# Weaving counted in TensorE's work, with a lag for each piece, and the scan's pair sum behind the second scan

## The chip, the cores and the metric

The kernel runs on one core of a Trainium2 chip. The metric is the time of one execution in microseconds on the device. The names in this text are those of the profile: PE is TensorE (matmuls, with PEld its weight loads), DVE is VectorE, ACT is ScalarE, POOL is GpSimd, and SP is SyncE, which here only issues DMAs. A line such as L539 is a line of the kernel before the change.

## The reference, cut to what matters

Eight samples of 512 tokens with 128 channels go through two layers, both with adaptive layer normalisation.

```python
# layer 0, for each of 8 samples x (512 x 128)
h  = LN(x) * (1 + ca) + sa
xn = LN(h) * ln1_w + ln1_b
#   causal attention, 16 heads of 8 channels
s  = mask(q @ k.T * 8 ** -0.5);  attn = softmax(s) @ v @ o_w + o_b
#   state space branch: 256 channels, 16 states
x_ssm, z = split(xn @ in_proj_w)
x_c = silu(causal_conv4(x_ssm));  dt = softplus(...);  Bm, Cm = ...
for t: state = exp(dt[t] * A) * state + (x_c[t] * dt[t]) * Bm[t]
       y[t] = sum over the 16 states of Cm[t] * state
ssm = ((y + x_c * D) * silu(z)) @ ssm_out_w
h  = h + alpha * attn + (1 - alpha) * ssm
h  = h + gelu(LN(h) @ ffn_w1) @ ffn_w2          # biases left out
x  = x + ga * h
hm = LN(x) * (1 + cb) + sb
#   mixture of experts: a shared one, and the 2 best of 8 by a router
logits = relu(hm @ Wr1) @ Wr2
x  = x + gb * (expert_shared(hm) + sum over e of weight[e] * expert_e(hm))
# layer 1: at each token, attention over the 8 samples (8 heads),
# then a channel mix: sigmoid(xr @ W_r) * (relu(xk @ W_k)**2 @ W_v)
```

An expert is `silu(hm @ W1 + b1) @ W2 + b2` with a hidden width of 512. All eight experts are computed for all tokens, and weighted with zeros where they were not chosen.

## The kernel before

All activations lie with the 128 channels on the partitions and the 512 tokens of one sample along the free axis. A loop over the samples b runs layer 0 as a software pipeline. Each stage is a Python generator which emits some instructions (a piece) and then yields a cost, a number that stands for the time of the piece. The function `weave` (L201) takes several such generators, each with a total cost and a stretch of the turn, for example 0 to 0.83, and always advances the one that is least far along its stretch. So the order of all instructions on PE, ACT and DVE is written out by hand, since the loop stands in a manual schedule for these three engines. POOL and SP are left to the framework's scheduler. Each engine executes its instructions in the order written and waits at an instruction until its operands are there.

In turn b these generators are woven:

- `attention(b)`: for each of four groups g of four heads, `projections` (queries and keys, L465 to L476), `maxima` (raw scores, L488 and L496, and their maximum on DVE, L520, into `mpad`), `shifts` (the negated maxima are transposed by TensorE as `mT`, L534, and added to the queries on DVE, L539), `exponentials` (scores again, now shifted, as `e` at L488, the mask added at L496, and the exponential on ACT, L558), `values` (L572), and `projected` (denominators L591, their reciprocal `rd` on DVE L599, broadcast by TensorE at L604, output projection L619 and L628).
- `ssm_scan(b)`, within 0 to 0.83 of the turn. It has 16 units, each of two states for half of the 256 channels. A unit has a product on DVE (`hs`, L783), two scans on DVE (L788), and a product with Cm on POOL (L792). The two states of the unit before are added by a pair sum on DVE (L764), and then to the running sum on POOL (L765). ACT computes the decays (L750). The tile `hs` has three buffers, the decays four, and the broadcast Bm and Cm rows, which SP loads by DMA, two each. `paced` ties each piece of the scan behind the DVE instruction of the attention that was marked last.
- `head(b+1)`: load, the first normalisation `lna`, and a second one, `ln1`.
- `attention2(b-2)`: layer 1's attention for one sample: a normalisation `lnc`, keys and values (L313, L320), queries (L329), and products and sums on POOL and DVE (L348 to L393).
- `ssm_inputs(b+1)` and the first seven pieces of `attention(b+1)`, at the turn's end.
- `finish(b-1)`: `tail`, which is the normalisation `ln2`, the feed-forward part (L834, L838), the normalisation `lnb` which gives `hm` (L283), and `routing` (first matmul L864); then `experts`, with nine experts of four matmuls L945, silu L949, four matmuls L960, and the weighted sum on DVE (`wb`, L968) and POOL (L971). The weights `wb` come by DMA (L957). L975 closes the sample.

A normalisation (`normalised`, L242 to L276) is a chain that leaves TensorE and returns three times: centring matmul L242, square and copy on ACT (L245, L247), variance matmul L254, addition of epsilon on DVE (L263), power -1/2 on POOL (L264), broadcast matmul L269, product on DVE (L276).

In PSUM there are three one-bank buffers for most matmuls, two for scores, and one accumulator.

Of the kernel before, what the change touches and what calls it, by code (L numbers as in the profile page):

```python
# [17 lines left out]
P = 128  # L18
# [5 lines left out]
NG = NH // 4  # L24
# [43 lines left out]
CST, NCST = _cols(_CONST)  # L68
MSK, NMSK = _cols(_MASK)


@with_exitstack
def kernel(
# [126 lines left out]
    def weave(*parts):  # L200

        live = []
        for k, (pieces, whole, begin, end) in enumerate(parts):
            live.append([begin, k, iter(pieces), (end - begin) / whole])
        while live:
            part = min(live)
            cost = next(part[2], None)
            if cost is None:  # L210
                live.remove(part)
            else:
                part[0] += cost * part[3]

# [22 lines left out]
    def normalised(src, name, lane, cost=0.9, n=T, ring=mm_tile, wait=0.0):  # L237


        mps = ring(f"{name}_m")[:, :n]  # L240
        to = mps if len(src.shape) == 2 else mps.rearrange("p (a b) -> p a b", a=src.shape[1])
        nc.tensor.matmul(to, lhsT=centre, rhs=src, start=True, stop=True)  # L242
        yield 0.2
        sq = lnp.tile([P, T], F32, tag=f"ln_s{lane}", name=f"{name}_s")
        nc.scalar.activation(sq[:, :n], mps, AF.Square)  # L245
        d = lnp.tile([P, T], F32, tag=f"ln_d{lane}", name=f"{name}_d")[:, :n]
        nc.scalar.copy(d, mps)  # L247
        yield 2 * cost - 0.2


        vps = ring(f"{name}_v")
        blocks = [(k, min(k, n - P)) for k in range(0, n, P)]
        for j, (_, lo) in enumerate(blocks):
            nc.tensor.matmul(  # L254
                vps[:, j : j + 1],
                lhsT=sq[:, lo : lo + P],
                rhs=mean_w,
                start=True,
                stop=True,
            )  # L260
        sd = lnp.tile([P, NTT], F32, tag=f"ln_r{lane}", name=f"{name}_r")
        nj = len(blocks)
        nc.vector.tensor_scalar(sd[:, :nj], vps[:, :nj], EPS, None, ALU.add)  # L263
        nc.gpsimd.tensor_tensor(sd[:, :nj], sd[:, :nj], mhalf[:, :nj], ALU.pow)  # L264
        yield cost + wait

        rps = ring(f"{name}_rb")
        for j, (k, lo) in enumerate(blocks):
            nc.tensor.matmul(  # L269
                rps[:, k : lo + P],  # L270
                lhsT=sd[:, j : j + 1].to_broadcast([P, P]),
                rhs=ident[:, k - lo :],
                start=True,
                stop=True,
            )
        nc.vector.tensor_mul(d, d, rps[:, :n])  # L276
        yield cost
        return d

    def layernorm(dst, src, scale, bias, name, lane, cost=0.9, n=T, ring=mm_tile, wait=0.0):  # L280

        d = yield from normalised(src, name, lane, cost, n, ring, wait)
        nc.scalar.activation(dst, d, AF.Identity, bias=bias, scale=scale)  # L283
        yield cost

# [16 lines left out]
    def attention2(s, at):  # L302
# [6 lines left out]
        for i0 in range(0, NB, 2):  # L309
# [14 lines left out]
            )  # L324
            yield 0.9
        ps = mm_tile(f"q2{s}")
# [11 lines left out]
        )  # L338
        yield 0.9
        yield from paced(attended(s, at, q, kv))  # L340

    def attended(s, at, q, kv):
# [13 lines left out]
        for i in range(NQ):  # L356
            pr = at.tile([P, NB, C], F32, tag="pr", name=f"pr{s}_{i}", bufs=2)
            nc.gpsimd.tensor_mul(  # L358
                pr, kv[:, :, 0, :], q[:, i, :].unsqueeze(1).to_broadcast([P, NB, C])
            )  # L360
            if last:
                summed(last)
            last = i, pr
            yield 1.6
        summed(last)
# [6 lines left out]
        nc.vector.tensor_sub(sc, sc, mx.unsqueeze(2).to_broadcast(s3))  # L372
        yield 1.6
        nc.scalar.activation(sc, sc, AF.Exp, scale=scale)
# [15 lines left out]
        for i in range(NQ):  # L390
# [9 lines left out]
            last = i, pr  # L400
            yield 1.6
        gathered(last)
# [19 lines left out]
    with ExitStack() as l0:  # L422
# [15 lines left out]
        def attention(b):  # L438
# [23 lines left out]
            def projections(g):  # L462
# [14 lines left out]
                qTs[g], kTs[g] = qT, kT  # L477
                yield 0.9

# [27 lines left out]

            def maxima(g, step):

# [7 lines left out]
                for qi, (a, n, _, _, _) in zip(STEPS[step], parts):  # L517
                    for pr in range(2):
# [8 lines left out]
                        )  # L527
                yield 0.6 + 0.25 * c0 / P

            def shifts(g):  # L530
# [9 lines left out]
                avs[g] = pacc.tile([P, T], F32, tag="acc", name=f"av{b}_{g}")  # L540
                yield 1.2

            exs = {}

            def exponentials(g, step):

# [13 lines left out]
                exs[g, step] = ex  # L560
                yield 0.6 + 0.25 * c0 / P

# [22 lines left out]
            def projected(g):  # L585
# [13 lines left out]
                nc.vector.reciprocal(rd, dps[:, : NTT * 4])  # L599
                yield 0.9  # L600
                rps = mm_tile(f"rb{b}_{g}")
# [9 lines left out]
                mark(nc.vector.tensor_mul(a, a, rps))  # L611
                yield 0.9

# [18 lines left out]
                yield 1.8  # L632

            yield from projections(0)
            for k in range(len(STEPS)):
                yield from maxima(0, k)
            for g in range(NG):
                yield from shifts(g)
                others = chain(
                    projections(g + 1) if g + 1 < NG else (), projected(g - 1) if g else ()  # L640
                )
                for k in range(len(STEPS)):
                    yield from exponentials(g, k)
                    next(others, None)
                    if g + 1 < NG and k:
                        alone(maxima(g + 1, k - 1))
                    values(g, k)
                    yield 0.85 + 0.25 * k
                    next(others, None)
                if g + 1 < NG:  # L650
                    yield from maxima(g + 1, len(STEPS) - 1)
                alone(others)
            yield from projected(NG - 1)

        def ssm_inputs(b, xn):
# [34 lines left out]
            for c in range(NDI):  # L690
                nc.scalar.activation(xc[c], xc[c], AF.Silu)
            yield 1.8
            ps = mm_tile(f"xd{b}")
# [9 lines left out]
            nc.scalar.copy(xd, ps[:80, :])  # L703
            yield 1.7
            bc = dram.tile([2, DS, T], F32, tag="bc", name=f"bc{b}")
# [5 lines left out]
            for c in range(NDI):  # L711
# [14 lines left out]
                nc.gpsimd.tensor_scalar(w, e, 1.0, 1.0, ALU.add, ALU.mult)  # L726
                yield 0.9

# [3 lines left out]
                dtx.append(w)  # L732
                yield 0.9
            yield 0.9
            for c in range(NDI):
# [5 lines left out]
        def ssm_scan(b, h, xc, zs, bc, dt, dtx):  # L741

            NN = 2
# [25 lines left out]
            for u, (n0, c) in enumerate(units):  # L769
# [15 lines left out]
                )  # L785
                yield 0.3
                for n in range(NN):
# [3 lines left out]
                    if n == NN - 1:  # L791
                        nc.gpsimd.tensor_mul(hs, hs, bcs[1])  # L792
                    yield 0.3
                    if n == 0 and summed:
                        add(*summed.pop())
                        yield 0.15
                summed.append((n0, c, hs))
            add(*summed.pop())
            yield 0.15
            for c in range(NDI):  # L800
                nc.gpsimd.tensor_mul(xc[c], xc[c], zs[c])
                yield 0.5
            yield 0.5
            ps = mm_tile(f"so{b}")
# [11 lines left out]
        def head(b):  # L816

            load_x(b)
            yield 0.5
            h = act.tile([P, T], F32, tag="h", name=f"h{b}", bufs=3)  # L820
# [5 lines left out]
        def tail(b, h):  # L826
# [5 lines left out]
            for m in range(NFF):  # L832
# [6 lines left out]
                hid.append(t)  # L839
            yield 3.4  # L840
            ps = mm_tile(f"f2{b}")
# [11 lines left out]
            )  # L853
            yield 3.4
            hm = act.tile([P, T], F32, tag="hm", name=f"hm{b}")
# [5 lines left out]
        def routing(b, hm):  # L861
# [4 lines left out]
            nc.scalar.activation(r1, ps[:32, :], AF.Relu, bias=cv("br1")[:32])  # L866
            yield 0.9
            ps = mm_tile(f"lg{b}")
# [23 lines left out]
            nc.vector.tensor_sub(lg, lg, wide(mx))  # L892
            yield 0.9
            yield 0.9
            nc.scalar.activation(lg, lg, AF.Exp)
# [13 lines left out]
            for _ in range(4):  # L909
                yield 0.9  # L910
            nc.scalar.activation(e2, e2, AF.Exp, scale=0.5)
# [22 lines left out]
        def experts(b, hm, we):  # L934
            acc = wk.tile([P, T], F32, tag="moe", name=f"moe{b}", bufs=1)
            wd = None
            for e in range(NE + 1):
# [5 lines left out]
                for m in range(NFF):  # L943
# [6 lines left out]
                    hid.append(t)  # L950
                yield 3.4
                if e == 1:
# [19 lines left out]
                else:  # L972
                    nc.vector.tensor_scalar(acc, ps, cv("b2", 0), None, ALU.add)
                yield 3.4
            nc.vector.scalar_tensor_tensor(  # L975
# [26 lines left out]
        with tc.manual_schedule(engines={mybir.EngineType.PE, mybir.EngineType.Activation, mybir.EngineType.DVE}):  # L1002
            behind = None
            for b in range(NB):
                h = ready[b][0]


                parts = [(ahead, 42.7, 0.0, 1.0)]
                parts.append((paced(ssm_scan(b, h, *inputs.pop(b))), 19.3, 0.0, 0.83))
# [4 lines left out]
                if b + 1 < NB:  # L1014
                    parts.append((after(b + 1), 8.0, 0.8, 0.97))
                    ahead = attention(b + 1)
                    parts.append((some(ahead, BEGUN), 7.3, 0.85, 1.0))
                if behind:
                    parts.append((behind, 91.5, 0.0, 1.0))
                weave(*parts)  # L1020
# [141 lines left out]
            def through(sp):  # L1162
# [6 lines left out]
            weave(  # L1169
                (behind, 91.5, 0.0, 1.0),  # L1170
                (
# [206 lines left out]
```

## Time and profile before

| | before |
|---|---|
| median of 3 runs | 2069.03 us (2065.26 to 2073.69) |
| the profiled execution | 2073.63 us |
| its span, first to last instruction | 2071.8 us |
| mean granted TensorE clock | 0.87 |
| until the loop starts to be full (b = 0) | about 57 us |
| one turn of the loop, b = 2 to 6 | about 228.6 us |

The shares of busy time on the page are averages over the whole span. A windows view gives the busy time of each engine in a stretch of the span, with the number of instructions in brackets, the granted clock (PEclk), the DMA share and its rate. In a list of waits, a row names the instruction that waited, with its engine, tile and line, then the instruction whose end released it, then the total time, the number of waits and the longest. In a timeline, a row has the start, the duration, the engine, the line, the tiles written and read, and in square brackets the idle time before it and its releaser.

### The profile page before, as it was taken

What the parts mean: (1) busy time and instruction counts of PE and PEld (TensorE: products, weight loads), DVE (VectorE), ACT (ScalarE), POOL (GpSimd) and SP (SyncE); (2) the same over time, 40 slices, a digit from 0 to 9 for tenths busy, and PEclk for the clock granted to TensorE, in tenths of its full rate; (3) what the DMA queues carried; (4) which work ended last, traced back from release to release, by engine and by line L of the source; (5) the groups of instructions that cost most, each with busy time, mean ns of one, the idle gap of its engine ahead of it and who ended that gap; (6) DMA issues with size and microseconds to landing.
All of it is one profiled execution on the core that took longest, in us unless ns stands there. A gap on an engine that the chain in (4) does not pass through costs nothing. (4 is left out here: it accounts for less than half of the span.)

```text
span 2071.8 us, 22824 instructions
## 1 busy us (share of the span) xinstructions
PE 1653.0 (80%) x8762; PEld 795.4 (38%) x8762; DVE 1441.0 (70%) x1648; ACT 985.2 (48%) x1413; POOL 1045.2 (50%) x539
## 2 busy tenths in 40 slices
PE   5765888888798887888789788888788768868864
PEld 3332343434343443334334443334333333344442
DVE  1798688647894798668885889568876889352255
ACT  2532555464544644455445554464536454423432
POOL 1566355535673566444772667355763567331131
PEclk9766789998999988999889898999889989968975
DMA  3220123121222122121212122121312122102200
GB/s 101 78 71 21 53 70 99 52 83 56 82 71 78 46 77 82 46 79 59 94 56 83 54 73 78 47 82 60 98 47 78 57 87 81 50 9 76 71 8 18
DMA packets 67405, 135.32 MB, mean 65 GB/s; under 512 B 7864, under 2 KB 23360, under 8 KB 67168
## 3 DMA queue, kind: packets, MB, share of 16 engines
q1 hardware_dynamic: 66816, 131.51, 20.5%
q10 hardware_dynamic: 288, 1.93, 0.3%
q8 instruction: 69, 1.13, 0.2%
q0 software_dynamic: 192, 0.42, 0.1%
q14 instruction: 40, 0.33, 0.1%
HBM read 129.24 MB, written 4.59 MB: 65 GB/s over the span
## 5 line engine op out<-in xcount | busy, mean ns | idle before, releaser
L788 DVE TENSOR_TENSOR_SCAN hs<-da,hs 128x512 f32<-128x512 f32 x256 | 442.8, 1732 | 6.5 <-DVE hs L783 0.5
L792 POOL TENSOR_TENSOR hs<-hs,bc 128x1024 f32<-128x1024 f32 x128 | 386.7, 3021 | 102.2 <-DVE hs L788 83.9
L945 PE MATMUL e<-hm,we 128*128 128x512 f32 x576 | 315.5, 679 | 84.7 <-DVE wb L968 45.6
L558 ACT ACTIVATE ex<-e 128x768 f32<-128x768 f32 (+1 forms) x192 | 158.8, 879 | 317.4 <-PE e L496 317.0
L765 POOL TENSOR_TENSOR xc<-xc,hs 128x512 f32<-128x512 f32 x112 | 199.1, 1778 | 200.1 <-DVE hs L764 200.1
L960 PE MATMUL e<-eh,we 128*128 128x512 f32 x576 | 272.1, 616 | 0.3
L783 DVE TENSOR_TENSOR hs<-bc,dtw 128x1024 f32<-128x1024 f32 x128 | 249.5, 1949 | 0.0
L949 ACT ACTIVATE eh<-e,vec_sb 128x512 f32<-128x512 f32 x288 | 188.5, 686 | 122.1 <-PE e L945 115.2
L520 DVE TENSOR_REDUCE mpad<-s 128x2 f32<-128x256 f32 (+3 forms) x256 | 193.9, 808 | 39.4 <-PE s L496 39.4
L971 POOL TENSOR_TENSOR moe<-moe,wb 128x512 f32<-128x512 f32 x64 | 94.2, 1472 | 223.8 <-DVE wb L968 223.8
L945 PEld LDWEIGHTS e<-hm,we 128*128 128x128 f32 x576 | 111.6, 214 | 241.2 <-issue 89.3
L488 PE MATMUL e<-qT,kT 32*128 32x512 f32 (+3 forms) x1024 | 135.0, 580 | 81.7 <-DVE qT L539 75.3
L750 ACT ACTIVATE da<-dtu,own 128x512 f32<-128x512 f32 x256 | 169.8, 719 | 12.6 <-POOL dtu L737 12.2
L960 PEld LDWEIGHTS e<-eh,we 128*128 128x128 f32 x576 | 108.5, 198 | 127.3 <-issue 113.8
L968 DVE SCALAR_TENSOR_TENSOR wb<-e,vec_sb,wb 128x512 f32<-128x512 f32 x64 | 47.7, 745 | 150.5 <-DMA wb<-wd 58.4
L488 PE MATMUL s<-kT,qT 32*128 32x128 f32 (+3 forms) x1024 | 134.7, 524 | 10.4 <-DVE mpad L520 5.5
L764 DVE TENSOR_TENSOR hs<-hs 128x512 f32<-128x512 f32 x112 | 93.7, 837 | 37.9 <-POOL hs L792 37.9
L393 POOL TENSOR_TENSOR pv<-kv,sc 128x1024 f32<-128x1024 f32 x32 | 62.2, 1952 | 108.4 <-DVE ao L387 90.6
L496 PEld LDWEIGHTS <-ident_b 128*128 128x128 bf16 x1024 | 63.4, 103 | 138.0 <-issue 131.3
L358 POOL TENSOR_TENSOR pr<-kv,q 128x1024 f32<-128x1024 f32 x32 | 88.5, 2777 | 33.6 <-DVE sc L348 18.6
L488 PEld LDWEIGHTS e<-qT,kT 32*128 32x128 f32 x1024 | 51.2, 214 | 139.3 <-DVE qT L539 84.7
L572 PE MATMUL av<-ex,va 128*32 128x512 f32 (+3 forms) x1024 | 99.1, 478 | 0.0
(277 smaller groups left out, 2488.5 us busy)
## 6 DMA issues: line engine op xcount, KB each, us to landing
bc<-bc SPq DMA_DIRECT2D x128, 512.0 KB, 3.8
we<-in_w_dram SPq DMA_DIRECT2D x144, 256.0 KB, 3.1
wb<-wd SPq DMA_DIRECT2D x64, 256.0 KB, 3.3
xin<-in_x_dram SPq DMA_DIRECT2D x8, 256.0 KB, 2.9
wa_sb<-in_wa_dram ACTq DMA_DIRECT2D x1, 1832.0 KB
kept<-ao SPq DMA_DIRECT2D x14, 128.0 KB, 2.5
ai<-kept SPq DMA_DIRECT2D x56, 32.0 KB, 2.2
out_dram<-xout SPq DMA_DIRECT2D x16, 96.0 KB, 2.3
```

The lines of the kernel that those rows point to most:

```text
L488: nc.tensor.matmul(tiles[i // 2][:, i % 2, c0 : c0 + n], lhsT=lhs[quadrant(i)], rhs=rhs[quadrant(i)], start=True, stop=False,)
L520: nc.vector.tensor_reduce(mpad[:, qi, 2 * pr : 2 * pr + 2, HD : HD + 1], tiles[pr][:, :, a : a + n], AX.X, ALU.max, negate=True,)
L558: nc.scalar.activation(t[:, :, :c0], tiles[pr][:, :, :c0], AF.Exp)
L572: nc.tensor.matmul(avs[g][quadrant(i), kj * P :], lhsT=va[:, kj, at : at + 32], rhs=ex[i // 2][:, i % 2, c0 : c0 + n], start=(kj == 0), st ...
L750: nc.scalar.activation(da[:, n, :], dt[c], AF.Exp, scale=A_sb[:, c, n0 + n : n0 + n + 1])
L765: nc.gpsimd.tensor_add(y, y, hs[:, 0, :])
L783: nc.vector.tensor_mul(hs, bcs[0], dtx[c].unsqueeze(1).to_broadcast([P, NN, T]))
L788: nc.vector.tensor_tensor_scan(hs[:, n, :], da[:, n, :], hs[:, n, :], 0.0, ALU.mult, ALU.add)
L792: nc.gpsimd.tensor_mul(hs, hs, bcs[1])
L945: nc.tensor.matmul(ps, lhsT=we1[:, m * P : (m + 1) * P], rhs=hm, start=True, stop=True)
L949: nc.scalar.activation(t, ps, AF.Silu, bias=cv("b1", e * NFF + m))
L960: nc.tensor.matmul(ps, lhsT=we2[:, m, :], rhs=hid[m], start=(m == 0), stop=(m == NFF - 1),)
```

## The change

A cost may now be a `Step`, a number with two more fields. `pe` is the TensorE work of the piece, equal to the cost if nothing is said, and `lag` is how much TensorE work should lie between this piece and the next one of the same generator. `weave` keeps a count `now` of the TensorE work issued. A generator whose lag has not passed is held back, by 0.06 of what is missing, against the others.

The pieces of the normalisations, of both attentions, of the router and of the experts get such lags. In the attention the next group's maxima and the pieces of `projected` and `projections` now come as pieces of their own in `weave`, through `one`, so the attention's whole grows from 42.7 to 64.3. Nearly all pieces of the scan have `pe` 0 and lag 0. The pair sum `add` now comes after the unit's second scan, not after its first.

```diff
+class Step(float):
+    def __new__(cls, cost, lag=0.0, pe=None):
+        self = super().__new__(cls, cost)
+        self.lag, self.pe = lag, cost if pe is None else pe
+        return self
+SOON = 0.06
...
     def weave(*parts):
         for k, (pieces, whole, begin, end) in enumerate(parts):
-            live.append([begin, k, iter(pieces), (end - begin) / whole])
+            live.append([begin, k, iter(pieces), (end - begin) / whole, 0.0])
+        now = 0.0
         while live:
-            part = min(live)
+            part = min(live, key=lambda p: (p[0] + SOON * max(0.0, p[4] - now), p[1]))
             cost = next(part[2], None)
             if cost is None:
                 live.remove(part)
-            else:
-                part[0] += cost * part[3]
+                continue
+            part[0] += cost * part[3]
+            now += getattr(cost, "pe", cost)
+            part[4] = now + getattr(cost, "lag", 0.0)
...
     def normalised(...):               # after L242, L247, L264, L276
-        yield 0.2
+        yield Step(0.2, 1.0, 0.9)
-        yield 2 * cost - 0.2
+        yield Step(2 * cost - 0.2, 1.8, 0.0)
-        yield cost + wait
+        yield Step(cost + wait, 5.0, 0.9)
-        yield cost
+        yield Step(cost, 1.6, 0.9)
...
             def maxima(g, step, lag=0.0):
-                yield 0.6 + 0.25 * c0 / P
+                yield Step(0.6 + 0.25 * c0 / P, 2.2 + lag)
             def shifts(g):
-                yield 1.2
+                yield Step(1.2, 3.0, 0.5)
             def projected(g):          # after rd, after rb
-                yield 0.9
+                yield Step(0.9, 2.2)
...
                 for k in range(len(STEPS)):
-                    yield from exponentials(g, k)
-                    next(others, None)
-                    if g + 1 < NG and k:
-                        alone(maxima(g + 1, k - 1))
+                    follows = g + 1 < NG and k
+                    yield from exponentials(g, k, 0.0 if follows or more else 3.2)
+                    yield from one(others, 0.0 if follows else 2.4)
+                    more = max(0, more - 2)
+                    if follows:
+                        yield from maxima(g + 1, k - 1)
                     values(g, k)
-                    yield 0.85 + 0.25 * k
-                    next(others, None)
+                    yield Step(0.85 + 0.25 * k)
+                    yield from one(others, 0.5)
                 if g + 1 < NG:
-                    yield from maxima(g + 1, len(STEPS) - 1)
-                alone(others)
+                    yield from maxima(g + 1, len(STEPS) - 1, 0.8)
+                yield from others
...
         def ssm_scan(...):
                 nc.vector.tensor_mul(hs, ...)
-                yield 0.3
+                yield Step(0.3, 0.0, 0.0)
                 for n in range(NN):
                     nc.vector.tensor_tensor_scan(hs[:, n, :], ...)
                     if n == NN - 1:
                         nc.gpsimd.tensor_mul(hs, hs, bcs[1])
-                    yield 0.3
-                    if n == 0 and summed:
+                    yield Step(0.3, 0.0, 0.0)
+                    if n == NN - 1 and summed:
                         add(*summed.pop())
-                        yield 0.15
+                        yield Step(0.15, 0.0, 0.0)
...
         def routing(b, hm):            # after the logits, and in the choice of experts
-            yield 0.9
-            yield 0.9
+            yield Step(1.8, 1.5, 0.4)
             for _ in range(4):
-                yield 0.9
+                yield Step(0.9, 0.0, 0.0)
         def experts(b, hm, we):        # after the first matmuls, after the second
-                yield 3.4
+                yield Step(3.4, 2.6)
-                yield 3.4
+                yield Step(3.4, 0.8)
...
-                parts = [(ahead, 42.7, 0.0, 1.0)]
+                parts = [(ahead, 64.3, 0.0, 1.0)]
-                    parts.append((after(b + 1), 8.0, 0.8, 0.97))
+                    parts.append((after(b + 1), 9.8, 0.8, 0.97))
-                    parts.append((behind, 91.5, 0.0, 1.0))
+                    parts.append((behind, 92.0, 0.0, 1.0))
```

## Prediction

> **What bounds the kernel now.** I read the page first: the span and the busy shares.
>
> ```profile
> span 2071.8 us, 22824 instructions
> ...
> PE 1653.0 (80%) x8762; PEld 795.4 (38%) x8762; DVE 1441.0 (70%) x1648; ACT 985.2 (48%) x1413; POOL 1045.2 (50%) x539
> ```
>
> TensorE has the most work, but 2071.8 - 1653.0 = 419 us of the span it does nothing. An average says little here, so the second view is the windows of one steady turn of the loop over the samples (b = 4, 228.6 us; turns 2 to 6 look alike), cut where the scan's last part begins:
>
> ```profile
> core 0: us, PE busy (x) PEld busy (x) DVE busy (x) ACT busy (x) POOL busy (x), PEclk, DMA share, GB/s
> 915.50:1074.40 158.90, 134.68 (x753) 64.88 (x753) 137.08 (x149) 83.37 (x117) 99.36 (x45) 0.87 0.22 68
> 1074.40:1144.10 69.70, 58.27 (x309) 25.83 (x312) 35.25 (x45) 35.48 (x49) 29.42 (x22) 0.95 0.24 74
> ```
>
> While the scan runs DVE is busy 137 of 159 us, nearly as long as PE (135). Afterwards it has slack. Over the turn PE is busy 193 and idle 35.6. The third view, TensorE's waits in that turn, says for what (us in total, times, longest):
>
> ```profile
> PE e L488 <- DVE qT L539: 9.6, 2, 6.9
> PE e L945 <- DVE wb L968: 6.1, 1, 6.1
> PE lna_rb L269 <- POOL lna_r L264: 4.6, 1, 4.6
> PE ln_rb L269 <- POOL ln_r L264: 4.1, 1, 4.1
> PE e L945 <- ACT eh L949: 3.9, 4, 2.1
> PE lnc_m L242 <- DVE xT L975: 3.4, 1, 3.4
> ```
>
> All are latencies of chains that leave TensorE and return: mask shift, expert sum, the normalisations' power. TensorE runs in the order written, so it stands whenever the work laid between two links is shorter than the latency. The kernel is bound by TensorE's work plus these chain stalls, and DVE can lengthen each chain, since DVE also runs in written order. The timeline of DVE and of TensorE at the turn's start shows both:
>
> ```profile
> 913.69 1.69 DVE L783 TENSOR_TENSOR hs<-bc,dtw 128x1024 f32<-128x1024 f32 x1
> 915.48 3.22 DVE L788 TENSOR_TENSOR_SCAN hs<-da,hs 128x512 f32<-128x512 f32 x2
> 919.07 0.16 DVE L263 TENSOR_SCALAR ln_r<-ln_v 128x4 f32<-128x4 f32 x1 [0.37 <-PE ln_v L254]
> ...
> 923.14 2.07 PE L269 MATMUL ln_rb<-cst_sb,ln_r 128*128 128x128 f32 x8 [4.11 <-POOL ln_r L264]
> ```
>
> The scan stands ahead of the tiny L263; the power on POOL follows, and then TensorE.
>
> **The change part by part.** It adds no work: the same 6049 PE, 1618 DVE, 544 POOL and 466 SP instructions are written. It moves them.
>
> *The hold-back.* A part is held by 0.06 of the lag still missing, counted in TensorE's work laid since. From the written orders with this trace's durations I worked out, for turn 4, the TensorE work laid between links (us, before to after): mask shift 2.2 to 2.9; second normalisation, variance to L269, 0 to 4.9; first normalisation 3.5 to 5.2; denominators to L604 2.5 to 6.0; expert sum to lnc_m 2.5 to 5.7. The sum over all chains of (latency less gap, where positive) falls from 296 to 253 us: by itself -43 us. Against: logits to the first expert, 6.0 to 2.15.
>
> *What the hold-back costs.* Nearly all the scan's pieces (L783, L788, the sums) and some routing pieces count zero TensorE work and zero lag. When others are held, they are what remains to issue, and a zero-cost piece does not advance the count that would release the others. So DVE's scan comes in bursts: runs of DVE work longer than 4 us, with no TensorE work needing it between, go from 8 (46 us in total, 3 over 6 us) to 15 (108 us, 8 over 6 us). The worst: 11.6 us at the turn's start, two scan units ahead of L263; 10.4 us ahead of the mul of the FFN-side normalisation (L276); 13.1 us near the scan's end. Queued behind those on DVE are the small links that TensorE awaits. Walked through turn 4, with before's stalls from the waits and after's from the order:
>
> - turn start, lnc_m: 3.4 to 2.0; a new wait at the x transpose, 0 to 1.1.
> - second normalisation: L263 comes 16.4 us after the mask-shift matmul instead of 9.3, its power 20.1 instead of 13.3; PE has more to do meanwhile: 4.1 to 7.0.
> - first normalisation: 4.6 to 6. Its PSUM slot then lets the next one wait, 0 to 3.3.
> - router's first matmul L864, which needs hm, behind the 10.4 us burst: 0 to 6.2.
> - first experts 2.8 to 5.1 (ACT, held behind the routing chain); expert sum L968 6.1 to 7.3.
> - denominators 2.0 to 0; mask shift of head group 2, 2.6 to 0; of group 3, 7.0 to 1.
> - end of the scan, L968 behind the 13.1 us burst: 0.4 to 6.4.
> - a few short waits: 2.6 to 1.0.
>
> Before sums to 35.6, after to about 46.4: +11 us a turn. A cruder measure agrees: the most by which DVE work required since the turn's start exceeds TensorE work laid, at L864, goes from 4.6 to 11.2 us. Turn 0 (54.1 to 62.4): +8. Turn 1 goes from 7.3 to 26.5, but before already stood 15.8 us there, which leaves at most +11. Turns 2 to 6: 5 x 11 = 55. Turn 7 (11.3 to 18.0): +6. After the loop the attention's end has less cover (about +5), a DMA wait of 5.0 gets covered: 0, bounds -6 to +6. Sum: 8 + 11 + 55 + 6 = +80.
>
> *Pair sum one operation later (L764).* Before it sat between the two scans; now behind the second, where POOL starts the multiply L792. The trace shows it both ways:
>
> ```profile
> 947.37 0.67 DVE L764 TENSOR_TENSOR hs<-hs 128x512 f32<-128x512 f32 x1
> 992.85 2.13 DVE L764 TENSOR_TENSOR hs<-hs 128x512 f32<-128x512 f32 x1
> ...
> 991.16 6.04 POOL L358 TENSOR_TENSOR pr<-kv,q 128x1024 f32<-128x1024 f32 x2
> ```
>
> Alone 0.67, beside a POOL multiply 2.13: at most 112 x 1.46 = +163 us on DVE. The Trainium skill ("SBUF — State Buffer", "Who interferes with whom") speaks harder against it: the port pair of DVE and GpSimd is an exclusive lock and the loser blocks fully. Then each sum waits out a multiply of 2.35 (the short form of L792): 112 x 2.35 = 263 us. The row's 1.46 is less and decides. And it is gross: L783 and L788, which stood beside that multiply until now, slow alike (1.21 alone, 2.0 to 2.2 beside), and the sum takes their place. Net I put 0, from below -38 (DVE's wait for POOL before L764, 37.9 us in 8 times, vanishes) to +7 a turn (0.5 for each of 14 sums). The cover is DVE's idle time, 56 us a turn, which lies mostly outside the bursts; without cover it is +7 x 8 = 56. L765 on POOL and its readers come one scan later; only the scan's end waits for them, and POOL is half idle.
>
> *Table loads.* The new order has 7 more on ACT (L558 +16, L949 +12, others -21). By the row 1283 ns each: 9.0 us. The skill's page "ScalarE: Activation LUTs" ("What ACT_TABLE_LOAD costs") adds a drain of about 1.38 us: 18.6. The rows of loads at L750 stand 0.6 us idle in 36, so no drain shows; 9.0, hidden, as ACT is 48% busy; uncovered +9.
>
> *The clock.* At a stall of 6.9 us TensorE's next 4 us ran at 0.50; after 3.4 us at 0.68:
>
> ```profile
> 1076.50:1083.40 6.90, 0.02 (x1) 0.00 (x0) 4.06 (x7) 0.00 (x0) 5.66 (x5) 0.89 0.12 38
> 1083.40:1087.40 4.00, 3.93 (x14) 1.70 (x15) 0.67 (x2) 1.48 (x2) 4.00 (x3) 0.50 0.00 0
> ...
> 913.20:917.20 4.00, 3.98 (x12) 1.20 (x12) 3.90 (x3) 2.83 (x6) 3.22 (x2) 0.68 0.30 68
> ```
>
> So a stall of 4 us or more costs some 2 us beyond itself. I count four such a turn before and four after: 0. The skill ("TensorE: Matmul & The Clock Gate", "Why this matters for your kernels") sets the limit at idle gaps above about 3 us: five before, six after, 7 x 2 = +14. The row decides; 14 stays in the range.
>
> The sum stands against the profiled execution: 2073.63 + 80 = 2154. That run is 4.6 above the median of the three, 2069.03; so 2149, said as **2150 us** (+3.9%).
>
> **The rivals.**
>
> *A. The hold-back does what it says; faster.* If ln_r on DVE still comes within some 9 us of the turn's start (no more than about 5 us of scan ahead of it), chain latencies stay what they were: -43 from the gaps, and where stalls fall under 4 us, some two a turn at 2 us, 2 x 2 x 8 = 32 of slow clock: 2150 - 80 - 75 = 1995. For it: every gap above grew but one, and PE's largest group of waits (L488 for L539, 75.3 us over the span) is aimed at. Against: the 11.6 us front of scan.
>
> *B. More than the bursts: pair sum uncovered.* +7 a turn on the DVE-bound stretch (137 of 159): 2150 + 56 = about 2205. For it: DVE is at 86% there. Against: the sum only trades places with other DVE work.
>
> *C. Given back.* Stalls move but their total stays: what the new L864 stall takes, mask shifts and denominators return, 2069 +- 10. It needs the bursts to cost half of what I walked. Measurement of this kernel cannot tell less than about 0.5% (10 us) from no change.
>
> **How the numbers follow.** Bursts (main) 0.61, B 0.12, A 0.19, C 0.08. The main case's own range is 2095 to 2195: bounds of the walk (half to one and a half of 80) with the clock's 14. The range for all is 2040 to 2215: it takes in main, B and C, and only the milder end of A. Slower by over 0.5%: 0.61 + 0.12 = 0.73; within: C, 0.08; faster: A, 0.19.
>
> **What would show it.** Right: in TensorE's waits a new row of several us a turn at the router's matmul L864 for ACT's hm, the wait for ln_r not smaller, L488 for L539 well under 75, L604 for rd near nothing; PE idle a turn near 46; the timeline with two scan units ahead of L263; L764's mean near 2 us, and DVE's 37.9 for POOL gone. Wrong: PE idle a turn under 36 with the same bursts (then the latencies hide behind the laid work), or L263 ahead of the second unit (A), or DVE busy over 180 a turn (B).

## The result, and the profile after

The changed kernel takes 2249.61 us (2235.83 to 2255.92, 4 runs) against 2068.03 us (2065.26 to 2073.69): a ratio of 1.0865, interval 1.0809 to 1.0921. It is slower, as forecast, but by 182 us where 81 were forecast. The profiled execution took 2251.09 us. Lines of the changed kernel are 12 to 24 higher than before's: L888 is the router's matmul (L864 before), L968 the experts' first matmuls (L945), L991 the weighted sum (L968), L816 the scan's multiply on POOL (L792).

The page of the changed kernel:

```profile
span 2249.3 us, 23007 instructions
...
PE 1696.0 (75%) x8762; PEld 800.5 (36%) x8762; DVE 1430.1 (64%) x1648; ACT 998.4 (44%) x1420; POOL 997.1 (44%) x539
```

TensorE runs the same 8762 matmuls, but is busy 43 us longer, which goes with its lower clock (0.842 against 0.870), and idle 553 us instead of 419, which is 134 more. DVE is busy 11 us less. So the work did not grow; the waiting did, and the same work took TensorE longer.

TensorE's longest waits, in all (us, times, longest), and under the dots those of before that belong to them:

```profile
PE e L968 <- DVE wb L991: 83.5, 28, 5.3
PE r L888 <- ACT hm L299: 56.2, 8, 14.5
PE e L968 <- ACT eh L972: 44.4, 29, 4.0
PE e L504 <- DVE qT L555: 34.5, 4, 20.6
PE lna_rb L285 <- POOL lna_r L280: 25.9, 7, 7.4
PE mT L550 <- DVE mpad L536: 24.2, 11, 15.6
PE ln_rb L285 <- POOL ln_r L280: 22.7, 8, 9.5
...
PE e L488 <- DVE qT L539: 75.3, 17, 7.3
PE e L945 <- DVE wb L968: 45.6, 7, 9.1
PE rb L604 <- DVE rd L599: 26.8, 11, 6.5
PE r L864 <- ACT hm L283: 6.1, 2, 4.0
```

The mask shift (L504 for qT) fell from 75.3 to 34.5 us, which is what the hold-back is for, and the wait for the denominators (L604, 26.8) is down to 0.3. In their place stand the router's wait for hm (56.2, from 6.1) and the experts' wait for the weighted sum (83.5 in 28 pieces, from 45.6 in 7).

The same turn as in the prediction (b = 4), cut at the scan's end:

```profile
1012.35:1186.78 174.43, 130.85 (x641) 59.89 (x644) 131.72 (x143) 80.35 (x112) 92.64 (x42) 0.83 0.20 61
1186.78:1261.95 75.17, 68.70 (x419) 30.80 (x420) 39.08 (x50) 39.64 (x55) 30.65 (x23) 0.95 0.24 71
```

The scan's stage is 174.4 us instead of 158.9, although both engines have less to do in it: TensorE 131 us, DVE 132. TensorE stands 43.6 us and DVE stands 42.7 (24.2 and 21.8 before). The bursts that the prediction read from the order are there. DVE's timeline has two scan units ahead of the small L279 (L263 before), which comes 17.3 us after the turn's first mask-shift matmul (at 1006.74); 9.9 us before the change:

```profile
1011.03 1.22 DVE L807 TENSOR_TENSOR hs<-bc,dtw 128x1024 f32<-128x1024 f32 x1
1012.35 2.34 DVE L812 TENSOR_TENSOR_SCAN hs<-da,hs 128x512 f32<-128x512 f32 x2
1014.60 1.20 DVE L807 TENSOR_TENSOR hs<-bc,dtw 128x1024 f32<-128x1024 f32 x1
1015.91 4.31 DVE L812 TENSOR_TENSOR_SCAN hs<-da,hs 128x512 f32<-128x512 f32 x2
...
1024.06 0.15 DVE L279 TENSOR_SCALAR ln_r<-ln_v 128x4 f32<-128x4 f32 x1
```

DVE's own waits in this stage are the view that the prediction did not draw; under the dots those of before:

```profile
DVE wb L991 <- DMA wb<-wd: 7.5, 1, 7.5
DVE mpad L536 <- PE s L512: 7.2, 2, 5.1
DVE rd L615 <- PE den L607: 6.9, 2, 6.2
DVE lg_sb L910 <- PE lg L894: 6.1, 1, 6.1
DVE lnc_d L292 <- PE lnc_rb L285: 4.0, 1, 4.0
DVE rst L919 <- ACT lg_sb L918: 3.9, 1, 3.9
...
DVE wb L968 <- DMA wb<-wd: 7.6, 1, 7.6
DVE lnc_d L276 <- PE lnc_rb L269: 3.5, 1, 3.5
DVE lg_sb L886 <- PE lg L870: 1.7, 1, 1.7
```

In before's stage maxima (`mpad`) and denominators (`rd`) did not make DVE wait, and the logits (`lg_sb`) did for 1.7 us. Now each engine waits for the other in turn.

Turn by turn, from the first mask-shift matmul of one sample to that of the next, before to after: turn 0, 176.8 to 204.4; turn 1, 212.5 to 246.4; turns 2 to 6 together, 1142.5 to 1239.5; turn 7 with all that follows, 472.2 to 490.6. That is +27.6, +33.9, +97.0 and +18.4. Of the 97.0 us TensorE is idle for 69 and busy for 28.

### The profile page after: what moved, and what is told of

The parts are those of the page before. It is cut to its first block, busy times and chain, and to the rows that moved or that the text cites. A ratio compares the mean times of both kernels' runs of the same rounds, so it can differ in the third digit from the quotient of the medians.

```text
span 2249.3 us, 23007 instructions
## 1 busy us (share of the span) xinstructions
PE 1696.0 (75%) x8762; PEld 800.5 (36%) x8762; DVE 1430.1 (64%) x1648; ACT 998.4 (44%) x1420; POOL 997.1 (44%) x539
## 5 line engine op out<-in xcount | busy, mean ns | idle before, releaser
L816 POOL TENSOR_TENSOR hs<-hs,bc 128x1024 f32<-128x1024 f32 x128 | 333.9, 2609 | 425.3 <-DVE hs L812 299.1
L968 PE MATMUL e<-hm,we 128*128 128x512 f32 x576 | 319.7, 685 | 143.0 <-DVE wb L991 83.5
L812 DVE TENSOR_TENSOR_SCAN hs<-da,hs 128x512 f32<-128x512 f32 x256 | 409.0, 1624 | 8.3 <-DVE hs L807 0.5
L536 DVE TENSOR_REDUCE mpad<-s 128x2 f32<-128x256 f32 (+3 forms) x256 | 195.6, 816 | 162.5 <-PE s L512 162.5
L807 DVE TENSOR_TENSOR hs<-bc,dtw 128x1024 f32<-128x1024 f32 x128 | 294.3, 2299 | 0.0
L972 ACT ACTIVATE eh<-e,vec_sb 128x512 f32<-128x512 f32 x288 | 190.2, 686 | 166.7 <-PE e L968 162.5
L574 ACT ACTIVATE ex<-e 128x768 f32<-128x768 f32 (+1 forms) x192 | 158.9, 880 | 224.3 <-PE e L512 223.8
L789 POOL TENSOR_TENSOR xc<-xc,hs 128x512 f32<-128x512 f32 x112 | 228.8, 2043 | 51.9 <-DVE hs L788 51.9
L968 PEld LDWEIGHTS e<-hm,we 128*128 128x128 f32 x576 | 109.7, 208 | 292.3 <-DVE wb L991 107.3
L774 ACT ACTIVATE da<-dtu,own 128x512 f32<-128x512 f32 x256 | 167.9, 719 | 29.1 <-DVE hs L812 27.6
L504 PE MATMUL s<-kT,qT 32*128 32x128 f32 (+3 forms) x1024 | 133.7, 517 | 33.3 <-ACT ex L574 20.2
L504 PE MATMUL e<-qT,kT 32*128 32x512 f32 (+3 forms) x1024 | 123.6, 551 | 44.2 <-DVE qT L555 34.5
L991 DVE SCALAR_TENSOR_TENSOR wb<-e,vec_sb,wb 128x512 f32<-128x512 f32 x64 | 47.2, 738 | 135.4 <-PE e L983 65.2
L588 PE MATMUL av<-ex,va 128*32 128x512 f32 (+3 forms) x1024 | 112.3, 522 | 2.3 <-ACT ex L574 2.2
L504 PEld LDWEIGHTS e<-qT,kT 32*128 32x128 f32 x1024 | 47.1, 211 | 138.3 <-issue 83.7
```

The costliest lines, as they stand in the source:

```text
L504: nc.tensor.matmul(tiles[i // 2][:, i % 2, c0 : c0 + n], lhsT=lhs[quadrant(i)], rhs=rhs[quadrant(i)], start=True, stop=False,)
L536: nc.vector.tensor_reduce(mpad[:, qi, 2 * pr : 2 * pr + 2, HD : HD + 1], tiles[pr][:, :, a : a + n], AX.X, ALU.max, negate=True,)
L574: nc.scalar.activation(t[:, :, :c0], tiles[pr][:, :, :c0], AF.Exp)
L588: nc.tensor.matmul(avs[g][quadrant(i), kj * P :], lhsT=va[:, kj, at : at + 32], rhs=ex[i // 2][:, i % 2, c0 : c0 + n], start=(kj == 0), st ...
L774: nc.scalar.activation(da[:, n, :], dt[c], AF.Exp, scale=A_sb[:, c, n0 + n : n0 + n + 1])
L789: nc.gpsimd.tensor_add(y, y, hs[:, 0, :])
```

## The experiments

The kernel before was run beside each group and lay between 2070.3 and 2070.7 us. Intervals are of the ratio to it.

**1. The parts of the change.** Only the pair sum moved, in the kernel before:

```diff
-                    if n == 0 and summed:
+                    if n == NN - 1 and summed:
```

> The kernel before, with only the pair sum moved behind the second scan; the order of TensorE's work stays that of before. Prediction's sum (the pair sum only trades places with other DVE work): 2069 within 15, L764's mean near 2 us, the mean of L783 or L788 smaller by as much, the wait of DVE for POOL before L764 gone. Rival (the pair sum beside POOL's multiply is paid in full on a DVE that is the bound while the scan runs): 7 us a turn, 2125. If it is the larger part of the 180 us, above 2150.

2052.26 us, 0.9918 (0.9898 to 0.9938): a gain of 18 us. L764's mean is 1.18 us, not 2. As expected it is a trade, and a slightly good one: the scans fell from 1732 to 1510 ns, the product L783 rose from 1949 to 2180, DVE's wait for POOL before L764 fell from 37.9 to 17.9, and POOL's multiply L792 fell from 3021 to 2532 ns.

```profile
L788 DVE TENSOR_TENSOR_SCAN hs<-da,hs 128x512 f32<-128x512 f32 x256 | 381.7, 1510 | 6.9 <-DVE hs L783 0.5 <-ACT eh L949 0.5 <-ACT da L750 0.3
L764 DVE TENSOR_TENSOR hs<-hs 128x512 f32<-128x512 f32 x112 | 132.2, 1180 | 17.9 <-POOL hs L792 17.9
```

The changed kernel with the pair sum back at `n == 0`:

> The changed kernel with the pair sum put back between the two scans. Pair sum a trade: 2250 within 15. Pair sum paid in full: 2190. If it was a gain that the rest ate up: 2270 or more.

2183.72 us, 1.0557 (1.0532 to 1.0581). So the same move costs 66 us in the changed kernel, while the order on TensorE and ACT is the same with and without it. This needed its own explanation (group 3). By turns, against before, this kernel has +20.7, +25.3, +42.4 (turns 2 to 6) and +18.5.

No hold-back:

```diff
-SOON = 0.06
+SOON = 0.0
```

> The changed kernel with SOON = 0: no piece is held back, while the attention's new pieces, the new totals and the pair sum stay. Theory of the bursts (the hold-back lets the scan's pieces run ahead in bursts, which stall the chains): runs of DVE work over 4 us in turn 4 fall from 15 (108 us) to 10 (51 us), so near the kernel before, 2070 to 2100, with the wait of TensorE for hm at the router under 10 us in all. Rival (the attention's new pieces move TensorE's work behind the scan's end, as turn 0 suggests, where 14 us more of it lie there): 2180 or more, with turn 0 still above 195 us.

2067.51 us, 0.9986 (0.9975 to 0.9996), and the wait for hm at the router is 2.1 us. What the change rearranges besides (the attention's new pieces, the new totals and costs) takes about 15 us (against e1_pair_only's 2052). The hold-back makes the loss: 182 us on top of this kernel. Turn 0 alone stays long, 185.9 us, so 9 of its 27.6 us come without any hold.

The scan counted:

```diff
-                yield Step(0.3, 0.0, 0.0)
+                yield 0.3          # and so for all six kinds of piece of ssm_scan
```

> The changed kernel with the scan's pieces counted in the clock of weave at their costs, instead of at zero. Theory that the zero count is what makes the bursts (nothing moves the count while only the scan is issued): bursts end sooner; in turn 4 runs of DVE work over 4 us go from 15 (108 us) to 11 (73 us), in turn 1 the largest run from 16.8 to 9.5 us: 2130 to 2190. Rival (the hold-back itself makes them, whatever the scan counts): 2230 to 2260.

2046.64 us, 0.9897 (0.9860 to 0.9934): 203 us less than the changed kernel, far more than expected. Its turn 4 (the profiled execution, 2035.84, is the fastest of its four):

```profile
909.40:1059.51 150.11, 120.64 (x702) 57.89 (x702) 128.78 (x145) 79.50 (x110) 92.89 (x42) 0.90 0.24 72
```

DVE stands 21.3 us in the stage, as before the change, and the stage is 8.8 us shorter than before.

**2. How the zero count hurts.** A lag for the scan itself:

```diff
-                yield Step(0.3, 0.0, 0.0)
+                yield Step(0.3, 1.2, 0.0)     # the pair sum: Step(0.15, 0.6, 0.0)
```

> The changed kernel with the scan's pieces still counted at zero, but with a lag of their own (1.2, the pair sum 0.6), so that they too are held back and spread over TensorE's work. Theory of the bursts (zero count hurts only because the scan alone is never held and so runs ahead): in turn 4 the runs of DVE work over 4 us fall from 15 (108 us) to 8 (51 us), as few as before: 2030 to 2080. Rival (what hurts is that the scan's pieces do not move the count, so that others stay held too long, however the scan is spread): 2180 to 2250.

2128.99 us, 1.0278 (1.0230 to 1.0327), between the two. By the written order the bursts in turn 4 are nearly as short as before the change (51 us in 8 runs; 46 in 8), yet a third of the loss remains, 59 of 180 us. In its turn 4 DVE is busy longer (140.7 us in the stage, POOL 99.3), and stands 27.1:

```profile
950.46:1118.25 167.79, 133.44 (x727) 62.48 (x726) 140.71 (x149) 86.87 (x119) 99.34 (x44) 0.88 0.22 68
```

So long bursts are not the whole cause.

A third of the hold, `SOON = 0.02`:

> The changed kernel with SOON = 0.02 instead of 0.06, the scan still counted at zero. Theory of the bursts: a third of the hold makes shorter bursts (turn 4: 9 runs over 4 us, 68 us, instead of 15 and 108; turn 1: the largest 10.7 instead of 16.8), so most of the loss is gone: 2060 to 2130. Rival (the zero count is what matters, whatever the size of the hold): 2200 to 2250.

2047.94 us, 0.9903 (0.9871 to 0.9936), with the scan still counted at zero. A zero count alone does no harm; it takes both the zero count and the full hold.

Counted, with the pair sum back at `n == 0`:

> The kernel of e4_scan_counts (2047) with the pair sum put back between the two scans. If the pair sum's move is a gain where bursts are short, as in the kernel before (18 us): 2055 to 2070. If it is a loss wherever pieces are held back, as in the changed kernel (66 us): 1980 to 2010.

2076.99 us, 1.0032 (1.0017 to 1.0046). Here the pair sum's move is worth 30 us of gain. Its loss in the changed kernel belongs to that order.

Work added on TensorE:

```diff
             ps = mm_tile(f"r1{b}")
+            for _ in range(3):
+                nc.tensor.matmul(ps, lhsT=centre, rhs=cw("f1"), start=True, stop=True)
...
         rps = ring(f"{name}_rb")      # for lna, from sample 1 on
+            for _ in range(2):
+                nc.tensor.matmul(rps[:, :n], lhsT=centre, rhs=cw("f1"), start=True, stop=True)
```

> The changed kernel with work added on TensorE and nothing else: ahead of the router's first matmul L888 three matmuls of 128x512 and ahead of the broadcast matmul L285 of lna two, into the same PSUM tile, which the real matmul then overwrites. About 5 us more of TensorE work a turn, laid into stalls of 5.7 and 3.7 us. Theory of the clock (a stall of 3 us or more is followed by about 4 us at half speed, so a filled stall saves up to 2 us): faster by 10 to 30 us, 2220 to 2240, with the clock after L888 near full. Rival (the clock is not what these stalls cost, the filler only takes time where there was none to spare): 2250 to 2280.

2251.50 us, 1.0894 (1.0858 to 1.0930): no difference from the changed kernel. The timelines of TensorE show the router's matmul and its neighbour, first in the changed kernel, then with the fill:

```profile
1083.49 1.92 PE L888 MATMUL r<-hm,wa_sb 128*32 128x512 f32 x2 [5.65 <-ACT hm L299]
1085.33 2.08 PE L258 MATMUL ln_m<-h,cst_sb 128*128 128x512 f32 x2
```

```profile
1077.91 4.40 PE L892 MATMUL r<-wa_sb,cst_sb 128*128 128x512 f32 x6 [4.80 <-DVE lnb_d L295]
1082.23 1.04 PE L893 MATMUL r<-hm,wa_sb 128*32 128x512 f32 x2
1083.21 1.13 PE L258 MATMUL ln_m<-h,cst_sb 128*128 128x512 f32 x2
```

The slow clock moved from the useful matmuls (1.92 to 1.04 us) to the fill, and those matmuls ran at full speed. Over the run the fill took 54 us of TensorE and all the rest 1658, which is 38 less than in the changed kernel. The time stayed. But the fill was also too long: `hm` was ready 76.7 us after the turn's start with and without it, and the router's matmul began at 76.75 us without it but at 80.23 with it. In six of the eight turns it began 3.4 to 4.3 us after `hm`. So a gain in speed and a delay may have cancelled, and this run does not tell what the lower clock costs.

**3. SP's queue.** SP's timeline in turn 4, changed kernel:

```profile
1119.70 0.33 SPq L954 DMA_DIRECT2D wd<-wT_sb  x1
1126.64 0.33 SPq L800 DMA_DIRECT2D bc<-bc  x1
1127.09 0.83 SPq L980 DMA_DIRECT2D wb<-wd  x2
```

and with the pair sum back (e2_pair_back):

```profile
1081.90 0.33 SPq L954 DMA_DIRECT2D wd<-wT_sb  x1
1084.51 0.80 SPq L980 DMA_DIRECT2D wb<-wd  x2
1090.95 0.32 SPq L800 DMA_DIRECT2D bc<-bc  x1
```

The scan's bc load waits for POOL's multiply to free its buffer:

```profile
SPq L800 <- POOL hs L816: 6.5, 1, 6.5
```

With the pair sum moved, the scheduler has put this load ahead of the experts' wb loads. They go out 7.4 us after the routing weights (wd) instead of 2.6, and DVE waits for them. Pinning this one order, on the changed kernel:

```diff
-                    nc.sync.dma_start(out=wb, in_=wd[...])
+                    ins = nc.sync.dma_start(out=wb, in_=wd[...])
+                    loads[:] = [ins.ins]
...
-                        nc.sync.dma_start(out=bcs[k], in_=bc[...])
+                        with tc.issue_after(loads[0]) if k == 1 and bool(loads) else nullcontext():
+                            nc.sync.dma_start(out=bcs[k], in_=bc[...])
```

> The changed kernel with one thing in SP's queue: the second DMA of the scan's rows (bc, L800) is issued behind the expert's wb load (L980) written last. The order on PE, DVE, ACT and POOL stays that of the changed kernel. There the pair sum's move put that bc load ahead of the first two wb loads; it waits 6.5 us for POOL's multiply, and DVE waits 7.5 us for wb. Theory (that queue is the loss of the pair sum in this kernel, 66 us): about 7 us a turn back, 2180 to 2215, DVE's wait for wb 51 to under 25 in all. Rival (the loss is the pair sum's contention with POOL, or its place on DVE): 2235 to 2255.

2207.23 us, 1.0663 (1.0635 to 1.0690): 42 us back, with the same order on the other four engines. DVE's wait for wb fell from 51.3 to 16.2 us. It is two thirds of the pair sum's 66 us; the rest was not traced. Most of the 42 shows as shorter busy time of TensorE: 1662.2 us instead of 1696.0, at a clock of 0.856, while its idle time fell by only 8.7 us.

```profile
PE 1662.2 (75%) x8762; PEld 786.7 (36%) x8762; DVE 1434.1 (65%) x1648; ACT 997.4 (45%) x1420; POOL 996.9 (45%) x539
```

The same on the kernel before, where a bc load also stands ahead of the wb loads, and these go out 6.4 us after wd:

> The kernel before, with the same one thing in SP's queue. It too has a bc load ahead of the first wb loads, and DVE waits 58.4 us in 8 times for wb, TensorE 45.6 us for L968. Theory: 3 to 6 us a turn back, 2025 to 2050. Rival (another wait closes in behind it): 2060 to 2075.

2021.61 us, 0.9767 (0.9744 to 0.9790): 49 us, more than expected. The two rows with the fix, and under the dots DVE's row without it:

```profile
DVE wb L972 <- DMA wb<-wd: 12.7, 7, 5.7
PE e L948 <- DVE wb L972: 1.3, 1, 1.3
...
DVE wb L968 <- DMA wb<-wd: 58.4, 8, 7.7
```

They were 58.4 and 45.6 us. TensorE's second longest wait in the kernel before came from a queue order on SP.

**4. What of the hold-back is left.** The attention's pieces as before, all else as changed:

```diff
-                    yield from one(others, 0.0 if follows else 2.4)
-                    if follows:
-                        yield from maxima(g + 1, k - 1)
+                    next(others, None)
+                    if g + 1 < NG and k:
+                        alone(maxima(g + 1, k - 1))
...
-                parts = [(ahead, 64.3, 0.0, 1.0)]
+                parts = [(ahead, 42.7, 0.0, 1.0)]
```

> The changed kernel with the attention's pieces as before (the next group's maxima and the projections issued within the pieces of exponentials and values, total 42.7), while the hold-back, the lags elsewhere and the zero count of the scan stay. Theory that DVE's new waits for TensorE (maxima 7 us and denominators 7 us a turn in the scan's stage, none before) come from the attention's new pieces being held: 2130 to 2170. Rival (the holds on the other chains, with the scan run ahead of them, make the loss by themselves; its runs of DVE work reach 24 us): 2220 to 2300.

2309.04 us, 1.1164 (1.1134 to 1.1193). The theory named there is wrong: DVE's waits for maxima and denominators are 174.8 and 65.0 us over the run (162.5 and 74.3 in the changed kernel), and the attention's fine pieces soften the hold-back's harm.

Half the hold, scan counted, `SOON = 0.03`:

> The scan's pieces counted at their costs and SOON = 0.03: half the hold-back. If a smaller hold is better also where the scan counts: 2030 to 2045. If the hold no longer matters once the scan counts: 2042 to 2052.

2024.11 us, 0.9775 (0.9754 to 0.9797): better again.

The normalisations' longest lag:

```diff
-        yield Step(cost + wait, 5.0, 0.9)
+        yield Step(cost + wait, 2.0, 0.9)
```

> The changed kernel with the normalisations' longest lag, behind the power on POOL, at 2.0 instead of 5.0; the zero count and SOON = 0.06 stay. Theory that this one long lag lets the scan run ahead: in turn 1 the most by which DVE's work leads falls from 35.7 to 26.0 us, in turns 0 and 4 hardly at all (70.2 to 70.4, 25.5 to 25.4), so turn 1 some 10 us shorter, the other turns as they are: 2230 to 2245. Rival (any lag does it, turn 1 too): 2245 to 2260. If the long lag alone makes the loss: under 2150.

2203.87 us, 1.0645 (1.0618 to 1.0669): 46 us back, more than expected, and not in turn 1 alone (246.4 to 240.0). Turns 2 to 6 give 23 us and the last one 14. This lag is part of the cause, not the cause.

Half the hold, counted, and SP's order pinned:

> Scan counted, SOON = 0.03 (2024) and the second bc load behind the expert's wb load in SP's queue. There DVE still waits 46 us for wb's DMA and TensorE 43.5 for the sum behind it. If the two gains add: 1975 to 1990. If they fall on the same stall: 2015 to 2025.

2021.43 us, 0.9774 (0.9748 to 0.9800). It does not add to the 2024 without the pin.

Pair sum moved and SP's order pinned, in the kernel before, no hold-back:

> The kernel before with the pair sum moved (2052 alone) and the bc load behind wb in SP's queue (2022 alone), without any hold-back. If the two add: 2000 to 2008. If the pair sum's gain was in SP's order only: 2018 to 2025. Beside j_best it tells what a mild hold is worth by itself.

2016.22 us, 0.9742 (0.9719 to 0.9765): the fastest of all, and 233 us below the changed kernel. Its turn 4:

```profile
892.17:1042.58 150.41, 130.72 (x753) 63.59 (x752) 138.10 (x149) 82.63 (x117) 93.08 (x44) 0.90 0.23 72
1042.58:1110.93 68.35, 58.23 (x306) 26.04 (x305) 36.48 (x46) 36.19 (x49) 30.21 (x22) 0.93 0.25 76
```

DVE stands 12.3 us in the stage, the least of the windows shown. The mild hold-back, with all that comes with it (2021), therefore brings nothing that a right queue order and the moved pair sum have not already brought. Beside the pin alone (2022) the pair sum's move gains only about 5 us, so most of its 18 us seem to lie on the stall that the pin removes.

## Why the prediction was right and wrong

**Which terms failed.** Of the forecast's terms two were put at nothing, and one was too small.

- *Pair sum, "Net I put 0".* In this order its move cost 66 us (2183.72 to 2249.61), above the largest bound given (56), and 42 of them through SP's queue, which the prediction did not look at.
- *The walk, +80.* With the pair sum back, the changed kernel is 113 us slower than before. By turns the walk said +8, +11, +55 and +6; e2_pair_back has +20.7, +25.3, +42.4 and +18.5. The steady turns were not underrated; turns 0 and 1 and the end came at more than twice what was said.
- *The clock, 0.* TensorE's busy time grew by 43 us. What it cost by itself stays open.

The first two add up to 179 us; the clock's share lies inside them.

**Right: the sign, and the walk at the turn's start.** The walk through turn 4 said that 25.6 us of stalls have come together at the router's matmul; 25.3 had. The single steps, predicted and measured: lnc_m 2.0 and 2.2; second normalisation 7.0 and 5.2; first normalisation 6 and 3.7; the slot behind it 3.3 and 3.9; the router 6.2 and 5.7. The sum is closer than its parts, which is partly luck: a wait of 2.7 us at L329, which the walk did not have, makes up for the two normalisations. Over the whole turn 46.4 us of idle time were said and 50.0 came. The stall foreseen at the scan's end (6.4) did not come; three waits of 3.2 to 3.6 us at experts for L991 came instead. The wait for `ln_r`, said to be not smaller, fell from 39.1 to 22.7 us over the run, but 19.4 us now stand at the matmul L488, which DVE's `ln_r` releases too. Up to the router, single stalls could be read from the written order to within 2 or 3 us.

**Wrong: only one direction of waiting was counted.** The walk took DVE as an engine that runs on without pause and asked when TensorE waits for it. But DVE's own waits in the scan's stage doubled. The scan's stages of turns 2 to 6, summed (us):

| | length | TensorE stands | DVE stands |
|---|---|---|---|
| before | 795 | 126 | 109 |
| changed | 867 | 221 | 209 |
| pair sum back (e2_pair_back) | 824 | 206 | 171 |
| scan counted (e4_scan_counts) | 752 | 148 | 108 |
| pair sum and pin, no hold (j_pair_bc) | 751 | 101 | 62 |

A reading that fits: held-back links leave DVE nothing to do but the scan, and when that has run ahead DVE stands at the next maxima, denominators or logits. The rows for maxima and denominators do not show it alone: in the 2024 us kernel (f_counts_soon03) they are 116.5 and 43.7 us over the run, against 39.4 and 19.8 before. In turn 0 the scan's end came 9 us later; the other 18 us are attention work of TensorE left behind it, with the waits that go with it. In turn 1 DVE stood 9.3 us at the feed-forward sum, 7.8 at the logits and 5.3 at the denominators.

**Wrong: SP's queue.** The sum followed the pair sum to POOL ("its readers come one scan later; only the scan's end waits for them") and stopped there. But the bc load waits for POOL to free its buffer, and other loads stand behind it on SP. Worth 42 us, more than half of the 80 that were forecast for everything. Before's own list already showed DVE waiting 58.4 us for the wb DMA; the longest row of SP's waits in that kernel is the bc loads' wait for POOL, and would have pointed to it:

```profile
SPq L776 <- POOL hs L792: 392.3, 48, 12.8
```

**Wrong: the clock at 0.** The prediction let only stalls of 4 us and more cost speed, and counted four of them after the change where its own list has five (7.0, 6, 6.2, 7.3 and 6.4). In the changed kernel's trace 23 stalls of 3.4 to 4 us were followed by 4 us at a mean clock of 0.54, and 53 stalls of 2 to 3.4 us by 0.63; in the 4 us ahead of 46 of these 53 the clock was above 0.95. TensorE is busy 43 us longer, 28 of it in turns 2 to 6. The Trainium skill's limit of about 3 us ("TensorE: Matmul & The Clock Gate", "Why this matters for your kernels") gave the estimate of +14: nearer, still short. What these 43 us are worth stays open. The fill won speed back and the time stayed, but it delayed the router's matmul; with the pin on SP, 34 of the 42 us came back as busy time. So they may not simply be added to the other terms, nor be called a mere sign of standing.

**Right for DVE's busy time, wrong in size: the pair sum on DVE.** L788's mean was forecast near 2 us; it is 0.81 (0.84 before), since POOL's multiply is often not running beside it. DVE's wait for POOL there went from 37.9 to 2.3 us. On DVE's busy time the move is small: +8 us in e1_pair_only, +17 from e2_pair_back to the changed kernel. The lock of the Trainium skill's page "SBUF — State Buffer" ("Who interferes with whom") gave the estimate of 263 us; nothing of that order is in the trace. (The page says "fully blocks" of DVE's two-port modes; of a `tensor_tensor` with both inputs in SBUF, which the pair sum is, it says that it contends with GpSimd's reads.)

Rival A, the hold-back doing what it says, exists in a milder form: with the scan counted and half the hold the kernel takes 2024. Rival B's time is nearer to the measured one than the main case, but its reason did not occur: DVE is busy 171 us in turn 4, not over 180. Rival C did not occur either; idle time grew by 134 us. The main case's upper bound, 2195, is too low by the prediction's own figures (2069 + 120 + 14 = 2203), and the result lies above both. What stays open is how the 159 us between the pinned changed kernel (2207) and the one with a third of the hold (2048) divide among the held chains. No single lag or piece explained more than 46 of them, and spreading the scan took 121 from the unpinned kernel without removing the loss.

## What to carry to other kernels

When a change reorders instructions by hand, draw the waits of every in-order engine against every other, both ways, and of the DMA queue too: a stage in which two engines each have 130 us of work can last 174. A count of one engine's work that ignores the other's pieces cost 203 us here under a strong hold; under a third of that hold the kernel was faster than before all the same (2048). The gain of one edit depends on the order around it: the pair sum's move was worth 18 us in the kernel before and 30 with the scan counted, and cost 66 in the changed kernel. Before moving any arithmetic, look at which load stands behind which in a DMA queue: here two lines there were worth 49 us.

## What was not expected of the hardware

TensorE ran slower after stalls as short as 2 us (53 of 2 to 3.4 us, mean clock 0.63 in the 4 us behind them), and a filled stall gave the speed back to the matmul behind it (1.04 instead of 1.92 us). The scan's product, its scan and the pair sum on DVE shift time among each other: from the kernel before to the changed one the scan's mean went from 1732 to 1624 ns and the product's from 1949 to 2299, while the three together took 786 and 793 us (793 in e1_pair_only too).
